# Attention with one quarter-array turn of eight families per step, full-array products alone between, and its first statistics and rows moved up a half round

## The chip, the cores and the metric

The kernel runs on one core of a Trainium2 chip. The core has a matrix engine (TensorE; in the profile PE for its matmuls and PEld for its weight loads), a vector engine (VectorE, DVE), an activation engine (ScalarE, ACT), a general engine (GpSimd, POOL) and a queue that issues most transfers (SyncE, SP). Each engine works through its own list of instructions, and semaphores make an instruction wait for another engine's. The metric is the time of one execution on the device in microseconds (us); lower is better. In the profile every instruction carries the line of the kernel that made it.

## The reference

Three residual blocks on x of shape 2 x 2048 x 256: a gated scan, a feed-forward network with ternary weights, an attention of second order, and the feed-forward network again. The change is in the attention and in what leads into it and out of it.

```
x = x + gated_scan(layernorm(x))
x = x + ffn(layernorm(x))
x = x + hla(layernorm(x))          # 16 heads of 64
x = x + ffn(layernorm(x))

def hla(x):                        # per batch and head
    q, k, v = x @ W_q, x @ W_k, x @ W_v
    for t:
        G   += k_t (k_t . C)       # with C before this t
        S   += k_t k_t^T
        C   += q_t v_t^T
        o_t  = q_t (S C - G)
    return o @ W_o
```

S C - G is the sum over i <= t of u_i v_i^T with u_i = S(i) q_i, so the attention is two linear attentions in a row: first u from q and the running sum S of k k^T, then o from q and the running sum M of u v^T.

## The kernel before

**Order.** The engines' orders are written out by hand: inside the attention each of PE, DVE, ACT and POOL executes its instructions in the order in which the program makes them. All tokens stay in on-chip memory (`x_sb`). `front` (from L555) runs the scan and the first feed-forward network, block by block; `attention` follows; then the second feed-forward network runs over the eight blocks of 512 tokens. Its first block is worked in among the last steps of the attention by the class `Last`.

**Steps.** The attention goes over 32 steps s: 16 chunks n of 128 tokens, each for batch 0 (even s) and batch 1 (odd s). Eight families of 32 matmuls belong to a step. Every matmul uses a quarter of the array (64 rows, 64 columns), four at a time:

- `inter(s, "S", "uT")`, `products(s, "kT", "p1")`, `intra(s, "S", "kN", "p1", "uT")` make u: what earlier chunks give, the masked products of k and q, what this chunk gives. `update(s, "kN", "kN", "S")` adds the chunk to S.
- `update(s, "uN", "vN", "M")` adds the chunk to M, and `inter(s, "M", "oT")`, `products(s, "uT", "p2")`, `intra(s, "M", "vN", "p2", "oT")` make o the same way.

DVE takes `products` out of PSUM under the mask (L838) and adds `update` to the sums (L901). `evict` (L870 on) copies u and o out of PSUM in three copies, on ACT or DVE. k and u are needed turned as well: `keys_out`/`units_out` transpose 32x32 squares on DVE (L260) and write them to DRAM, `turn_rows` reads them back (both on SP's queue), and `turn_end` (for u: `units_end`) copies them into place on ACT (L931).

**Products.** Between the quarter-array families PE runs full-array (128x128) matmuls: `outward` (L912), which multiplies o by W_o in two halves of 3 and 5, and the projections. `Seven` computes one projection (k, q or v) of a whole chunk of both batches with seven products instead of eight; `go(1)` to `go(7)` issue them, `go(0)` is an addition alone. They share two or three PSUM banks: `X` holds product 1; product 6 is added into the same bank after ACT has copied product 1 out, then 7 after ACT has copied 6 out, then 4 after DVE has added 7 elsewhere. k is projected in even steps (seven products), q and v in odd ones (fourteen). X and Z of k and q lie in the two banks of the ring "uT", which also holds the two banks of `inter(s, "S", "uT")`; those of v lie in the ring "oT". Four more banks are the ring "ps".

**The order inside a step before.** The families are spread over four places of a step, two at a time, and projections and `outward` lie between them: `inter` and `products` for u; then both `intra`; then `update` of S and M; then `inter` and `products` for o of the step before. ACT's units_end(s-1) lies in an even step at its start, in an odd step between the evictions and the projections; the rows of the next chunk (`norm_rows`, L195) or their turned copy (`norm_end`, L313) come at the end of a step, after `k.go(4)` or `q.go(4)`.

**Lead-in.** The first chunk's rows are normalized and turned through DRAM by three functions, `attention_stats`, `attention_rows` and `attention_turned`, called from `front` as `then[0]`, `then[1]`, `then[2]` in the last of its eight feed-forward rounds. `a_(4)` adds the scan's result of unit 4 to `x_sb` (transposes on PE, L424, and two additions on DVE) ahead of the first round.

## Time and profile before

| what | value |
|---|---|
| time, median of 3 runs | 1082.48 us (1080.03 to 1083.65) |
| the profiled execution's own time | 1081.18 us |
| its span, first to last instruction | 1079.3 us |
| PE busy in the span | 1057.5 us (98%) |
| DVE, ACT, POOL busy | 681.0, 596.4, 175.5 us (63%, 55%, 16%) |
| mean granted TensorE clock | 0.995 |
| `outward` (L912), 512 instructions | 124.0 us busy |
| masked evictions (L838), 128 instructions | 82.1 us busy, 682 ns each |
| turned copies kT and uN (L931), 32 and 31 | 66.7 and 64.6 us busy, 2085 ns each |
| k squares to DRAM and back, median from issue to landing | 3.5 us out, 2.9 us back |
| u squares to DRAM and back | 3.3 us out, 3.1 us back |

The span runs from the first to the last instruction of the profiled execution; the device time is a little longer. "Busy" of PE counts a matmul from its start to the modelled end, so neighbours overlap, and PE's start-to-start distances say more than its busy time. In an f32 row of the timeline "x2" or "x8" counts instruction records: a product of k or v is 2 records of 512 columns, one of q 8 records of 128, a quarter-array family 64 records. The attention's steps run from about 236 us to 956 us of the span; the first of them starts its quarter-array work at 259.9 us.

### The profile page before, as it was taken

The numbers are of one execution on the slowest core, as the hardware profiler recorded it, in microseconds if no ns is written. First come the engines' busy times: TensorE is split into PE (matmuls) and PEld (weight loads), VectorE is DVE, ScalarE is ACT, GpSimd is POOL, SyncE is SP. The second block draws the span as 40 slices with busy tenths as digits, with TensorE's granted clock in tenths as the row PEclk, the third lists the DMA queues.
The fourth block names the chain that finished last, engine by engine and source line by source line (L and its number), as shares of the span: only waits on it lengthen the run. The fifth ranks groups of instructions, "written<-read, shape, count | busy, mean of one in ns | idle before, by whom it ended". The sixth has DMA issues, their size and how long they took to land. (4 is left out here: it accounts for less than half of the span.)

```text
span 1079.3 us, 43538 instructions
## 1 busy us (share of the span) xinstructions
PE 1057.5 (98%) x20024; PEld 817.6 (76%) x20024; DVE 681.0 (63%) x1041; ACT 596.4 (55%) x826; POOL 175.5 (16%) x290
## 2 busy tenths in 40 slices
PE   9989999979999999999999999999999999999998
PEld 7557779866677777777777777777777777789987
DVE  7965556544665757667657576676675665645554
ACT  4446666854555455544554545545545455447875
POOL 3422223831011011010110100101101011013120
PEclk9999999999999999999999999999999999999999
DMA  9220000002433424324333243342342443211011
GB/s 329 96 78 1 1 2 1 1 20 80 139 100 120 135 73 135 128 72 139 102 120 127 79 134 107 95 139 101 121 134 75 133 122 116 62 60 37 24 40 39
DMA packets 71463, 97.58 MB, mean 90 GB/s; under 512 B 7280, under 2 KB 58864, under 8 KB 71024
## 3 DMA queue, kind: packets, MB, share of 16 engines
q1 hardware_dynamic: 69664, 92.43, 26.0%
q8 instruction: 157, 2.57, 1.0%
q10 hardware_dynamic: 1584, 2.36, 0.9%
q14 instruction: 26, 0.21, 0.1%
q0 software_dynamic: 32, 0.00, 0.0%
HBM read 50.99 MB, written 43.78 MB: 88 GB/s over the span
## 5 line engine op out<-in xcount | busy, mean ns | idle before, releaser
L838 DVE TENSOR_TENSOR p<-hp,mask 128x512 f32<-128x512 f32 x128 | 82.1, 682 | 84.9 <-PE hp L832 84.9
L912 PE MATMUL hy<-wo,oT 128*128 128x256 f32 x512 | 124.0, 385 | 0.9 <-PE hqT_X L773 0.5
L204 DVE TENSOR_TENSOR hl<-h,hh 128x1024 fp32r<-128x1024 f32 x60 | 74.2, 1240 | 64.7 <-ACT hh L203 64.6
L912 PEld LDWEIGHTS hy<-wo,oT 128*128 128x128 f32 x512 | 93.6, 190 | 20.3 <-issue 7.7
L502 ACT ACTIVATE h<-h,b_sb 128x512 f32<-128x512 f32 x120 | 77.7, 682 | 49.5 <-PE h L496 49.4
L730 POOL TENSOR_TENSOR S<-xnT 128x128 f32<-128x128 f32 x30 | 13.8, 461 | 512.5 <-ACT xnT L313 512.5
L874 ACT COPY uT<-huT 128x512 f32<-128x512 f32 x32 | 18.7, 585 | 129.4 <-PE huT L863 129.4
L195 ACT ACTIVATE xn<-x_sb,nb,rs 128x256 f32<-128x256 f32 x124 | 65.2, 591 | 18.8 <-POOL nb L181 18.8
L901 DVE TENSOR_TENSOR S<-S,hS 128x512 f32<-128x512 f32 x60 | 41.2, 686 | 42.5 <-PE hS L889 39.5
L931 ACT COPY kT<-rawkT 128x1024 f32<-128x1024 f32 x32 | 66.7, 2085 | 0.0
L260 DVE STREAM_TRANSPOSE sqkT<-kN 128x1024 f32<-128x1024 f32 x32 | 65.8, 2056 | 1.3 <-ACT kN L809 1.2
L260 DVE STREAM_TRANSPOSE squN<-uT 128x1024 f32<-128x1024 f32 x31 | 63.6, 2052 | 4.0 <-ACT uT L876 3.5
L931 ACT COPY uN<-rawuN 128x1024 f32<-128x1024 f32 x31 | 64.6, 2085 | 1.0 <-ACT uT L876 0.7
L203 ACT CAST hh<-h 128x1024 fp32r<-128x1024 f32 x60 | 63.0, 1050 | 1.9
L518 PE MATMUL o<-w2r,hh 128*128 128x256 f32 x256 | 62.0, 284 | 0.0
L518 PE MATMUL o<-w2r_back,hh 128*128 128x256 f32 x248 | 60.3, 284 | 0.9 <-DVE x_sb L527 0.9
L518 PE MATMUL o<-w2r,hl 128*128 128x256 f32 x256 | 60.8, 279 | 0.0
L518 PE MATMUL o<-w2r_back,hl 128*128 128x256 f32 x248 | 59.9, 282 | 0.0
L496 PE MATMUL h<-xh,w1r 128*128 128x512 f32 x128 | 58.6, 458 | 0.0
L809 ACT COPY vN<-hvN_X 128x512 f32<-128x512 f32 x16 | 9.4, 585 | 78.8 <-PE hvN_X L778 78.8
L163 DVE BATCH_NORM_STATS2 st<-x_sb 128x6 f32<-128x256 f32 x128 | 51.4, 402 | 2.3 <-DMA x_sb<-in_x_dram 2.3
L783 DVE TENSOR_TENSOR kN<-kN,hkN_Y 128x512 f32<-128x512 f32 x16 | 11.0, 686 | 64.9 <-ACT kN L792 64.9
(221 smaller groups left out, 2504.7 us busy)
## 6 DMA issues: line engine op xcount, KB each, us to landing
dsqkT<-sqkT SPq DMA_DIRECT2D x32, 512.0 KB, 3.5
rawkT<-dsqkT SPq DMA_DIRECT2D x128, 128.0 KB, 2.9
dsquN<-squN SPq DMA_DIRECT2D x31, 512.0 KB, 3.3
rawuN<-dsquN SPq DMA_DIRECT2D x124, 128.0 KB, 3.1
out_dram<-x_sb SPq DMA_DIRECT2D x15, 256.0 KB, 2.3
x_sb<-in_x_dram SPq DMA_DIRECT2D x7, 512.0 KB, 9.0
dsqxn<-sqxn SPq DMA_DIRECT2D x14, 256.0 KB, 3.7
rawxn<-dsqxn SPq DMA_DIRECT2D x56, 64.0 KB, 2.5
```

Source lines behind the costliest of these rows:

```text
L163: nc.vector.bn_stats(st[:, c, :], x_sb[:, g, :])
L195: nc.scalar.activation(xn[:, c, :], x_sb[:, g, :], AF.Identity, bias=nb[:, c : c + 1], scale=rs[:, c : c + 1],)
L203: copy(hi, src)
L204: nc.vector.tensor_tensor(lo, src, hi, ALU.subtract)
L260: nc.vector.transpose(to, src)
L496: nc.tensor.matmul(ph, lhsT=w1r[:, d, f * P : (f + 1) * P], rhs=r[:, d, :], start=(d == 0 and k == 0), stop=(d == ND - 1 and k == 1),)
L502: nc.scalar.activation(h[:, f % 2, :], ph, AF.Gelu, bias=b1_sb[:, f : f + 1])
L518: nc.tensor.matmul(to, lhsT=h[f // 2][:, f % 2, c * P : (c + 1) * P], rhs=w2r[:, f, :], start=(f == 0 and k == 0 and c % 2 == 0), stop=(f ...
L838: nc.vector.tensor_tensor(d[s][nm][:, h], banks[h], mask8, ALU.mult)
L901: nc.vector.tensor_tensor(t, prev, banks[c], ALU.add)
L912: nc.tensor.matmul(py, lhsT=d[s]["oT"][:, p, :], rhs=wo[:, p, :], start=(p == 0), stop=(p == NPR - 1),)
L931: act(t, d[s]["r" + nm].rearrange("p t q -> p q t"))
```

## The change

Each step starts with all its quarter-array work in one stretch, written as `quarters(s)`; the work for o lags by two steps instead of one (`inter`, `products`, `intra` of s-2 beside those of u of s). After it come the projections, `outward` (both halves of s-2, moved into the same step), the squares and the rows. All evictions of o but the last go on ACT. `update` loses its `between` hook, `products`, `inter` and `evict` take another ring or tag for the last step. The last steps and `Last` are laid out anew: the last two o's are made in one final stretch, and `second_squares` follows it.

```
+        def quarters(s):
+            inter(s, "S", "uT")
+            products(s, "kT", "p1")
+            if s >= 1:
+                units_end(s - 1)
+                update(s - 1, "uN", "vN", "M")
+            if s >= 2:
+                inter(s - 2, "M", "oT")
+                products(s - 2, "uT", "p2")
+            intra(s, "S", "kN", "p1", "uT")
+            evict(s, "uT")
+            if s < NS - 1:
+                update(s + 1, "kN", "kN", "S")
+            if s >= 2:
+                intra(s - 2, "M", "vN", "p2", "oT")
+                evict(s - 2, "oT")
...
         for s in range(NS):
             first, n = s % 2 == 0, s // 2
             more = n + 1 < CPB
-            inter(s, "S", "uT")
-            products(s, "kT", "p1")
...
+            quarters(s)
+            if more and first:
                 k = Seven(n + 1, "kN", "uT")
-                k.go(2)
...
+                k.go(1, 2)
                 units_out(s)
                 turn_rows(s, "uN")
+                k.go(5)
                 if n + 2 < CPB:
+                    stats = norm_stats(norm_pool, pair(n + 2), bias=True)
+                else:
+                    last.stats()
+                k.go(0)
+                outward_(s - 2, 0)
+                k.go(6, 7)
                 turn_end(s + 1, "kT")
...
-                k.go(*((6, 3, 7) if s > 0 else (3,)))
...
+                outward_(s - 2, 1)
+                k.go(3)
+                keys_out(s + 2)
+                turn_rows(s + 2, "kT")
                 k.go(4)
                 if n + 2 < CPB:
                     xn = norm_rows(norm_pool, pair(n + 2), stats)
                 else:
                     last.rows()
+                    last.weights(True)
+            elif more:
+                q, v = Seven(n + 1, "qT", "uT"), Seven(n + 1, "vN", "oT")
+                q.go(2, 1)
+                v.go(2, 1)
+                units_out(s)
+                turn_rows(s, "uN")
+                if n + 2 < CPB:
+                    raw = norm_squares(pool, pair(n + 2), [xn], 2, "xraw", 1)
+                last.part()
+                for i in (5, 0, 6):
+                    q.go(i)
+                    v.go(i)
+                last.part()
+                outward_(s - 2, 0)
+                turn_end(s + 1, "kT")
+                q.go(7)
+                v.go(7)
+                last.part()
+                keys_out(s + 2)
+                turn_rows(s + 2, "kT")
+                outward_(s - 2, 1)
+                q.go(3)
+                v.go(3)
+                last.part(None)
+                q.go(4)
+                v.go(4)
+                if n + 2 < CPB:
+                    xnT = norm_pool.tile([P, ND, B * P], FP, tag="xnT", bufs=1, name=f"xnT{n + 2}")
+                    pairs[n + 2] = norm_end(raw, xnT)
+                    pair_sums(n + 2)
+                else:
+                    last.weights(False)
+                    last.turned()
+            elif first:
+                last.begin()
+                last.fill(2)
+                units_out(s)
+                turn_rows(s, "uN")
...
+                turn_end(s + 1, "kT")
+                last.second_stats()
...
             else:
+                last.fill(1)
                 outward(s - 2, 0)
-        last.out()
-        last.second_squares()
-        outward(NS - 3, 1)
+                outward(s - 2, 1)
+                units(s)
+                last.second_rows()
+                last.fill(1)
+        inter(NS - 2, "M", "oT")
+        products(NS - 2, "uT", "p2")
+        update(NS - 1, "uN", "vN", "M")
+        inter(NS - 1, "M", "oT", "uT")
+        products(NS - 1, "uT", "p2", "p1")
         intra(NS - 2, "M", "vN", "p2", "oT")
         evict(NS - 2, "oT")
...
+        intra(NS - 1, "M", "vN", "p2", "oT")
+        evict(NS - 1, "oT", dve, "uT")
+        last.second_squares()
+        last.out(2)
```

Ahead of the first step, v's product 4 and the turning of the next chunk's rows move out of step 0, and the second chunk of k is read back earlier:

```
         keys_out(1)
+        turn_rows(1, "kT")
...
         v.go(3, 7)
+        v.go(4)
+        pairs[1] = norm_turned(norm_pool, pair(1), xn, bufs=1)
+        pair_sums(1)
```

In `front`, `a_(4)` goes behind the first products and the first matmuls of round 0 (for that `scan_room` is split into `scan_gate` and `scan_pair`), and the three calls for the attention's first chunk move up by about half a round:

```
         t_(5)
-        a_(4)
         two_rings()
...
-                for _ in range(4):
+                for j in range(4):
                     run(products, 1)
                     run(steps, 1)
+                    if i == 0 and j == 0:
+                        a_(4)
...
-            if not more:
+            if i == NB - 2:
                 then[0]()
...
-            if not more:
+            if i == NB - 2:
+                then[1]()
+            elif not more:
                 wo = const.tile([P, NPR, D], FP, tag="wo", name="wo")
                 nc.sync.dma_start(out=wo, in_=w_o.rearrange("(c p) e -> p c e", p=P))
-                then[1]()
+                then[2]()
...
-                else:
-                    then[2]()
```

More of the change, by code (lines that the diff above doesn't have):

```diff
@@ L376, in scan_part @@
         pa, pkv, pq = ps
-        a, kq = scan_room(pool, g0, e)
+        a, kq = scan_gate(pool, g0, e), scan_pair(pool, g0, e)
         nc.scalar.activation(a[:, :nt], pa, AF.Sigmoid)
@@ L392, in product @@
             return pq
-        room = [scan_room(pool, g0, e) for e in range(ND)]
+        gate = [scan_gate(pool, g0, e) for e in range(ND)]
         for e in range(ND):
-            nc.scalar.activation(room[e][0], product(2, e), AF.Sigmoid)
+            nc.scalar.activation(gate[e], product(2, e), AF.Sigmoid)
         yield
         for e in range(ND):
-            a, kq = room[e]
+            a, kq = gate[e], scan_pair(pool, g0, e)
             kv = product(1, e)
@@ L406, in scan_steps, with scan_gate, scan_pair @@
             yield
-    def scan_room(pool, g0, e):
-        a = pool.tile([P, BT], FP, tag="a", name=f"a{g0}_{e}")
-        return a, pool.tile([P, 2, BT], FP, tag="kq", name=f"kq{g0}_{e}")
+    def scan_gate(pool, g0, e):
+        return pool.tile([P, BT], FP, tag="a", name=f"a{g0}_{e}")
+    def scan_pair(pool, g0, e):
+        return pool.tile([P, 2, BT], FP, tag="kq", name=f"kq{g0}_{e}")
     def scan_line(pool, g0, e, nt, a, kq, kv, last):
@@ L822, in attention, with products @@
         mask8 = mask2.unsqueeze(1).to_broadcast([P, NPR, CH])
-        def products(s, left, nm):
+        def products(s, left, nm, tag=None):
             b, n = steps[s]
@@ L835, in products, with inter @@
                         )
-            d[s][nm] = pool.tile([P, 2, NPR, CH], FP, tag=nm, bufs=1, name=f"{nm}{b}_{n}")
+            d[s][nm] = pool.tile([P, 2, NPR, CH], FP, tag=tag or nm, bufs=1, name=f"{nm}{b}_{n}")
             for h in range(2):
                 nc.vector.tensor_tensor(d[s][nm][:, h], banks[h], mask8, ALU.mult)
-        def inter(s, sums, nm):
+        def inter(s, sums, nm, ring=None):
             b, n = steps[s]
-            banks = [bank([P, NPR, CH], f"h{nm}{b}_{n}_{c}", nm) for c in range(2)]
+            banks = [bank([P, NPR, CH], f"h{nm}{b}_{n}_{c}", ring or nm) for c in range(2)]
             for p in range(NPR):
@@ L868, in intra, with evict @@
                         )
-        def evict(s, nm, copy=act):
+        def evict(s, nm, copy=act, tag=None):
             b, n = steps[s]
             banks = d[s][nm + "b"]
-            t = pool.tile([P, NPR, P], FP, tag=nm, bufs=2 if nm == "uT" else 1, name=f"{nm}{b}_{n}")
+            tag = tag or nm
+            t = pool.tile([P, NPR, P], FP, tag=tag, bufs=2 if tag == "uT" else 1, name=f"{nm}{b}_{n}")
             copy(t[:, :, halves[0]], banks[0])
@@ L877, in evict, with update @@
             d[s][nm] = t
-        def update(s, left, right, sums, between=None):
+        def update(s, left, right, sums):
             b, n = steps[s]
@@ L894, in update @@
             for c in range(len(banks)):
-                if between and c == 1:
-                    between()
                 t = state.tile([P, NPR, DK], FP, tag=f"{sums}{b}", bufs=3, name=f"{sums}{b}_{n}_{c}")
@@ L977, in attention, with outward_ @@
         v.go(3, 7)
+        v.go(4)
[17 more added lines that the diff above has]
+                evict(s - 2, "oT")
+        def outward_(s, half):
+            if s >= 0:
+                outward(s, half)
         for s in range(NS):
@@ L980, in attention @@
             more = n + 1 < CPB
-            inter(s, "S", "uT")
-            products(s, "kT", "p1")
-            if first and n + 2 < CPB:
-                stats = norm_stats(norm_pool, pair(n + 2), bias=True)
-            elif s == NS - 4:
-                last.stats()
-            elif s == NS - 2:
-                last.second_stats()
-            if s == 0:
-                v.go(4)
-                pairs[1] = norm_turned(norm_pool, pair(1), xn, bufs=1)
-                pair_sums(1)
-            if s % 2 == 1 and more:
-                q, v = Seven(n + 1, "qT", "uT"), Seven(n + 1, "vN", "oT")
@@ L995, in attention @@
-            if s == 1:
-                q.go(2)
-                v.go(2)
-                keys_out(s + 1)
-            elif s % 2 == 1 and s + 1 < NS:
-                keys_out(s + 1)
-            if s == 2:
-                k = Seven(n + 1, "kN", "uT")
-                k.go(2)
-            if first and s > 0:
-                units_end(s - 1)
-            if s < NS - 1:
-                last.part()
-            if s >= 3:
-                outward(s - 3, 1)
-            intra(s, "S", "kN", "p1", "uT")
@@ L1011, in attention @@
-            if s >= 2:
-                intra(s - 2, "M", "vN", "p2", "oT")
-            if s + 1 < NS:
-                turn_rows(s + 1, "kT")
-            evict(s, "uT")
-            if not more:
-                if not first:
-                    evict(s - 2, "oT", dve)
-                last.begin(first)
-                fill = last.fill
-                fill(1)
-                if first:
-                    evict(s - 2, "oT", act)
-                else:
-                    units_end(s - 1)
-                    units(s)
-                fill(1)
-            elif first:
-                if s != 2:
-                    k = Seven(n + 1, "kN", "uT" if s > 0 else "oT")
-                    k.go(2)
-                k.go(1)
-                if s >= 2:
-                    evict(s - 2, "oT")
-                else:
-                    units_out(s)
-                    turn_rows(s, "uN")
-                k.go(0, 5)
-                if s == 0:
-                    k.go(6)
-            else:
-                if s >= 2:
-                    evict(s - 2, "oT", dve)
-                if s > 1 or not more:
-                    units_end(s - 1)
+            quarters(s)
@@ L1046, in attention @@
+            if more and first:
+                k = Seven(n + 1, "kN", "uT")
+                k.go(1, 2)
                 units_out(s)
                 turn_rows(s, "uN")
+                k.go(5)
                 if n + 2 < CPB:
-                    raw = norm_squares(pool, pair(n + 2), [xn], 2, "xraw", 1)
-                if s > 1:
-                    q.go(2)
-                    v.go(2)
-                for part in (q, v) if s > 1 else (v, q):
-                    part.go(1)
-                if s == NS - 3:
-                    last.part()
@@ L1057, in attention @@
-                q.go(0, 5)
-                v.go(0, 5)
-                if s == 1:
-                    units_end(s - 1)
-                q.go(6)
-                v.go(6)
-            last.part()
-            if s == NS - 1:
-                last.second_rows()
-            if s + 1 < NS:
-                update(s + 1, "kN", "kN", "S", None if s > 0 else lambda: k.go(7))
-            if s >= 1:
-                update(s - 1, "uN", "vN", "M")
-            if s == NS - 1:
-                update(s, "uN", "vN", "M")
@@ L1072, in attention @@
-            if first and not more:
-                turn_end(s + 1, "kT")
-            if not more:
-                fill(1)
-            elif first:
-                k.go(*((6, 3, 7) if s > 0 else (3,)))
-            else:
-                v.go(7)
-                q.go(7)
-                if s == NS - 3:
-                    last.part()
-                v.go(3, 4)
-                q.go(3)
-            last.part()
-            if first and s > 0:
-                units_out(s)
-            if more:
-                turn_end(s + 1, "kT")
@@ L1090, in attention @@
-            if s >= 1:
-                inter(s - 1, "M", "oT")
-                products(s - 1, "uT", "p2")
-            if not more:
-                fill(1)
-            elif first:
+                    stats = norm_stats(norm_pool, pair(n + 2), bias=True)
[4 more added lines that the diff above has]
+                k.go(6, 7)
+                turn_end(s + 1, "kT")
+                outward_(s - 2, 1)
+                k.go(3)
@@ L1100, in attention @@
                     last.rows()
-            else:
-                q.go(4)
-            if not first and s + 2 < NS:
-                keys_out(s + 2)
-            if first and s > 0:
-                turn_rows(s, "uN")
-            if not first and n + 2 < CPB:
-                xnT = norm_pool.tile([P, ND, B * P], FP, tag="xnT", bufs=1, name=f"xnT{n + 2}")
-                pairs[n + 2] = norm_end(raw, xnT)
-                pair_sums(n + 2)
-            elif s == NS - 3:
-                last.turned()
@@ L1113, in attention @@
-            if s == NS - 4:
-                last.weights(True)
-            last.part()
-            if s == NS - 3:
-                last.part(None)
-                last.weights(False)
-            if s >= 2:
-                outward(s - 2, 0)
-        last.out()
-        last.second_squares()
-        outward(NS - 3, 1)
+                    last.weights(True)
[37 more added lines that the diff above has]
+                turn_rows(s, "uN")
+                last.part()
+                outward(s - 2, 0)
+                last.fill(2)
+                turn_end(s + 1, "kT")
+                last.second_stats()
+                last.part()
+                outward(s - 2, 1)
+                last.fill(2)
+                last.part(None)
+            else:
+                last.fill(1)
+                outward(s - 2, 0)
+                outward(s - 2, 1)
+                units(s)
+                last.second_rows()
+                last.fill(1)
@@ L1124, in attention @@
+        inter(NS - 2, "M", "oT")
[3 more added lines that the diff above has]
+        products(NS - 1, "uT", "p2", "p1")
         intra(NS - 2, "M", "vN", "p2", "oT")
         evict(NS - 2, "oT")
-        last.out()
-        inter(NS - 1, "M", "oT")
-        products(NS - 1, "uT", "p2")
+        intra(NS - 1, "M", "vN", "p2", "oT")
+        evict(NS - 1, "oT", dve, "uT")
+        last.second_squares()
+        last.out(2)
@@ L1129, in attention @@
         outward(NS - 2, 0)
         outward(NS - 2, 1)
-        intra(NS - 1, "M", "vN", "p2", "oT")
-        evict(NS - 1, "oT")
-        last.out()
         last.second_turned()
+        last.out(2)
         outward(NS - 1, 0)
@@ L1212, in halves_room, with begin, out @@
                 return t[:, 0], t[:, 1]
-            tag = (None, "kN", "qT", "vN")[a]
-            return [self.room(tag, [P, 2, BT], f"{t}{a}_", FR) for t in ("hh", "hl")]
-        def begin(self, first):
-            if first:
-                self.hid = Hidden(self.g0, self.halves_room)
-                self.steps = ffn_in(
-                    self.g0, self.rhs, self.hid,
-                    lambda a: const.tile([P, 2, BT], FP, tag="wv_t", name=f"h_last{a}"),
-                )
+            tags = ("kN", "kN") if a == 1 else ("qT", "vN")
+            return [self.room(tag, [P, 2, BT], f"{t}{a}_", FR) for t, tag in zip(("hh", "hl"), tags)]
+        def begin(self):
+            self.hid = Hidden(self.g0, self.halves_room)
+            self.steps = ffn_in(
+                self.g0, self.rhs, self.hid,
+                lambda a: const.tile([P, 2, BT], FP, tag="wv_t", name=f"h_last{a}"),
+            )
         def fill(self, n):
             run(self.steps, n)
-        def out(self):
+        def out(self, n):
             if not hasattr(self, "outs"):
-                self.outs = ffn_out(self.g0, self.hid, True, "uT")
-            run(self.outs, 1)
+                self.outs = ffn_out(self.g0, self.hid, True, "oT")
+            run(self.outs, n)
     by_hand = {
```

## The prediction

> **What bounds the kernel now.** First the busy times: PE works nearly the whole span, the others a little over half of it, so only PE's own work and its waits count. Then PE's waits, longest first.

> ```profile
> PE 1057.5 (98%) x20024; PEld 817.6 (76%) x20024; DVE 681.0 (63%) x1041; ACT 596.4 (55%) x826; POOL 175.5 (16%) x290
> ...
> PE hkN_Y L778 <- ACT xnT_first L313: 5.9, 1, 5.9
> PE py L424 <- DVE kq L380: 3.2, 1, 3.2
> PE hoT L849 <- DVE M L901: 2.1, 1, 2.1
> ...
> PE hM L889 <- ACT uN L931: 1.0, 1, 1.0
> ```

> All waits stand in the lead-in and the last steps; from 350 to 850 us PE waits for no other engine. Third, the timeline of an odd step, to price a turn from full-array to quarter-array work and back.

> ```profile
> 543.95 1.02 PE L778 MATMUL hvN_X<-wv_t,S 128*128 128x512 f32 x2
> ...
> 544.90 1.02 PEld L889 LDWEIGHTS hS<-kN 64*64 64x64 f32 x64 [0.76 <-issue]
> 544.91 1.16 PE L889 MATMUL hS<-kN 64*64 64x64 f32 x64
> ...
> 545.83 1.03 PEld L889 LDWEIGHTS hM<-vN,uN 64*64 64x64 f32 x64
> 545.89 1.11 PE L889 MATMUL hM<-vN,uN 64*64 64x64 f32 x64
> ...
> 546.93 1.12 PE L778 MATMUL hvN_X<-wv,S 128*128 128x512 f32 x2
> ...
> 547.89 1.05 PE L773 MATMUL hqT_X<-S,wq 128*128 128x128 f32 x8
> ```

> From one product's start (543.95) to the end of the next one's issue (547.89) are 3.94 us. Two 512-column products follow each other elsewhere at 0.86, a second family's weight loads start 0.93 after the first's. 3.94 - 2 x 0.86 - 2 x 0.93 leaves 0.36 us for one turn. Last the granted clock, in windows around the two long waits (columns: window, length, PE busy and records, clock, DMA share, GB/s).

> ```profile
> 56.50:59.90 3.40, 0.82 (x8) 1.00 0.00 0
> 59.90:63.30 3.40, 2.81 (x7) 0.50 0.00 0
> 234.00:237.40 3.40, 1.68 (x15) 1.00 0.20 77
> ...
> 240.80:247.70 6.90, 6.09 (x10) 0.51 0.00 0
> ```

> Each long wait is followed by a stretch at half clock.

> **What the change removes.** *Turns:* the trace has 131 stretches of quarter-array matmuls; the new order of PE has 34. 97 x 0.36 = 34.9 us. That is PE's own time, so it counts in full.
> *Lead-in of the attention:* the rows, squares and transfers of the first chunk are issued a half round earlier, behind SP work of that round only; round 7 takes some 15 us on PE (220.6 to 235.7) and the chain from the squares to the copy `xnT_first` took 6.5 us (233.95 to 240.47), so it is hidden. The wait of 5.9 goes. The four groups that ran at half clock started 1.87, 1.71, 1.70 and 1.27 us apart instead of 0.86 to 0.89: 3.1 more. What the earlier rows add on ACT (1.09) and DVE (1.11 and statistics) lies beside PE's round 6; uncovered it would cost 2.2.
> *`a_(4)`:* behind two gate products (4 records each, 3.4 us) and four FFN matmuls, its transposes find kq ready. About 0.4 us for xnT remains of the 3.2, and 1.1 of half clock goes: 3.8. Together 12.8.
> *Waits of the last steps that are laid out anew:* 2.1 + 1.0 + 0.5 + 0.2, and 0.7 for qT in step 2: 4.5.

> **What it adds: product 7 behind product 6.** Before, product 3 stood between:

> ```profile
> 523.30 1.12 PE L778 MATMUL hkN_X<-wk_t,S 128*128 128x512 f32 x2
> ...
> 524.27 1.02 PE L778 MATMUL hkN_Z<-wk,S 128*128 128x512 f32 x2
> ...
> 524.47 0.58 ACT L800 COPY kN<-hkN_X 128x512 f32<-128x512 f32 x1 [1.07 <-PE hkN_X L778]
> ...
> 525.12 1.10 PE L778 MATMUL hkN_X<-wk,S 128*128 128x512 f32 x2
> ```

> Product 7 starts 0.07 after ACT's copy of 6; without product 3 PE would have been there at 524.27. `k.go(6, 7)` makes that 0.85 us of waiting in each of 15 even steps: 12.8. `outward`'s first half, which could cover it, stands before product 6.

> **What it adds: uN comes last on ACT.** In the new order ACT has, one after the other: the copy of the stretch's last product (4), the rows (even) or their turned copy (odd), then `units_end`. PE has after product 4 only `inter` and `products`, then `update` of M, which reads uN.

> ```profile
> 528.18 1.13 PE L778 MATMUL hkN_X<-wk_t,xnT 128*128 128x512 f32 x2
> ...
> 529.35 0.59 ACT L809 COPY kN<-hkN_X 128x512 f32<-128x512 f32 x1 [2.31 <-PE hkN_X L778]
> 529.83 1.09 ACT L195 ACTIVATE xn<-x_sb,nb,rs 128x256 f32<-128x256 f32 x2
> ...
> 555.27 1.15 ACT L313 COPY xnT<-rawxn 128x512 f32<-128x512 f32 x1
> ...
> 556.32 2.09 ACT L931 COPY uN<-rawuN 128x1024 f32<-128x1024 f32 x1
> ```

> Product 4, not being the first of its stretch, ends 1.02 after its start. Then 0.05 to the copy, 0.48 to the next instruction (529.35 to 529.83), 1.05 for rows or turned copy (555.27 to 556.32), 2.09 for uN, 0.05 back to PE: 4.74. PE would be at the update after 0.95 (product with turn) + 0.98 + 0.93 = 2.87. Wait: 1.87 us. In odd steps 0.7 of it falls earlier, because `inter` wants the bank that product 4 is still copied from; the sum is the same. Everything behind the waiting matmul on PE, five families, slides with it. Nothing covers it: in steps 2 to 28, 27 x 1.87 = 50.5. Bounds: 1.6 if the copies follow closer than shown, 2.1 if each hop costs 0.1: 43 to 57.

> Is uN's transfer in time? u's evictions end 9.4 after the step's start, DVE's S additions 10.1, its squares 12.2; out and back took 528.92 to about 536.4 here (issue at 533.3 plus 3.1), 7.4, so it lands at 19.6; an even step lasts 20.0 and ACT asks at 21.6. Two us of slack, in odd steps seven. DVE's other duties (masks, M, S) end 0.3 to 1 us before PE wants them.

> **Ends.** Step 0: product 4 of v right behind product 7 waits for DVE's addition (0.9), `intra` for the mask (1.5). Step 1: its uN has a short step before it (squares until 8.4, landing 15.4 to 15.9, copy to 17.5, update wanted at 13.5): 4.0 to 4.5. Step 29 has twice as many rows, 2.9; step 30 casts instead, 1.0. In step 31 squares of u stand behind the FFN's split on DVE, so uN is some 5.4 late, and `outward` waits 1.4 for o. The final stretch: `inter` of the last o waits for mask and M addition (1.8), its `intra` for the mask (0.5), `out` 0.3. `second_squares` now starts behind the last eviction: transfer (8.6 from 943.06's squares on, by the rows there), cast 2.05 and difference 2.05 end about 2 us after PE wants them. Sum 22; these are rough, 12 to 30.

> **Sum.** 1079.3 - 34.9 - 12.8 - 4.5 + 12.8 + 50.5 + 22 = 1112.4 us of span. The execution took 1.9 more than its span: 1114.3, and the median of the runs stands 1.3 above the profiled execution: I say 1115. Per pair of steps it is 43.1 now, 45.6 then: six turns less (2.1), two uN waits and one product wait more (4.6).

> **The clock.** A window with 0.82 of 3.40 us busy was followed by half clock, one with 1.68 busy was not. A wait of 1.87 leaves at least 1.53 busy, between the two and near the second, so I take full clock; at the other end all 27 waits would cost 1.7 us each, 46. [...]

> **Rivals.**
> - *ACT is in time, and the turns decide (8%).* For it: ACT is busy 55% only, and PE waited for uN once so far, 1.0 us. Against: before, uN's copy ended six to eight us ahead of its reader (558.4 for 566.1); now it stands behind product 4 in the same list. It would give 1112.4 - 50.5 = 1061.9, or 1065 as a median. The point is a wait of about 0.65 us: 1112.4 - 1079.3 = 33.1 too much, 33.1 / 27 = 1.2 less than 1.87.
> - *Break-even (2%)*: the wait comes out at about that point.
> - *The half of it (6%)*: waits of 0.8 to 1.2, 1086 to 1098.
> - *The waits take the clock down as well (13%).* For it: the window above with 0.82 busy. Against: 1.68. With a quarter to all of the 27: 1127 to 1161.
> - *The turns stay.* Excluded: the order of PE shows 34 stretches.

> **Chances and range.** My forecast, 1098 to 1127, has 71%. Slower by over 0.3% (what a measurement of this kernel can tell from no change) is forecast, half and clock: 90%; same 2%; faster 8%. The range 1098 to 1130 takes in both ends of the uN wait (-7, +6), of the product wait (0.65 to 0.9: -3, +1), of the ends (-10, +8) and the lowest part of the clock case.

> **What will show it.** Right: PE's list of waits is led by hM waiting for ACT's uN, near 55 us in some 30 waits; hkN_X waits for ACT's kN 15 times, 12.8 us; no wait for `xnT_first`, no half clock at 240 us. Wrong: hM waits for a transfer, or for 0.6 and less; a clock below 1.00 between 260 and 900 us; steps of a pair less than 44 us apart.

## The result, and the profile after

| | before | after |
|---|---|---|
| time, median of 4 runs each | 1082.89 us (1080.03 to 1083.65) | 1236.88 us (1235.78 to 1240.47) |
| span of the profiled execution | 1079.3 us | 1238.7 us |
| PE busy | 1057.5 us (98%) | 1059.5 us (86%) |
| mean granted clock | 0.995 | 0.988 |
| first quarter-array matmul of the attention | 259.89 us | 246.56 us |
| a pair of steps in the middle (after: 560.5 to 614.9 us) | 43.1 us | 54.4 us |

The ratio is 1.1433, with an interval of 1.1402 to 1.1465. The prediction said slower and gave 1115, with 1130 as its upper end: the direction held, the size did not. PE has the same matmuls as before and is as busy as before; 14% of the span is now waiting. The list of PE's waits of the kernel after (columns: total us, times, longest) shows for whom:

```profile
PE hM L893 <- ACT uN L933: 43.5, 31, 4.6
PE hS L893 <- issue: 26.1, 15, 2.5
PE hoT L866 <- issue: 25.6, 16, 2.2
PE hp L835 <- issue: 21.3, 15, 1.9
PE huT L866 <- issue: 20.2, 14, 1.9
PE hkN_X L781 <- ACT kN L803: 11.5, 15, 0.8
PE huT L852 <- ACT kN L812: 9.4, 14, 0.7
```

The lines for uN and for the copies of k are the predicted ones. Those that end in "issue" are not: there the profile shows nothing that PE waited for. Over the whole kernel they are 98.4 us in 69 waits; before, they were 1.3 us in 3:

```profile
PE hp L832 <- issue: 0.6, 1, 0.6
PE hqT_Y L773 <- issue: 0.5, 1, 0.5
PE hy L912 <- issue: 0.2, 1, 0.2
```

The timeline of an even step after shows where they lie (columns: start, length, instruction; in brackets the idle time before it):

```profile
560.50 1.16 PE L852 MATMUL huT<-qT,S 64*64 64x64 f32 x64
561.48 1.11 PE L835 MATMUL hp<-qT,kT 64*64 64x64 f32 x64
564.24 1.16 PE L893 MATMUL hM<-vN,uN 64*64 64x64 f32 x64 [1.65 <-ACT uN L933]
565.23 1.11 PE L852 MATMUL hoT<-qT,M 64*64 64x64 f32 x64
566.16 0.65 PE L835 MATMUL hp<-qT,uT 64*64 64x64 f32 x32
568.04 0.64 PE L835 MATMUL hp<-qT,uT 64*64 64x64 f32 x29 [1.24 <-issue]
...
569.50 0.64 PE L893 MATMUL hS<-kN 64*64 64x64 f32 x31
571.50 0.64 PE L893 MATMUL hS<-kN 64*64 64x64 f32 x29 [1.36 <-issue]
```

They do not stand at the head of a family, as the wait for uN at 564.24 does, but in its middle, and they stand a fixed number of records apart: the matmul at 571.50 is the 128th after the one at 568.04. Every matmul here has its own weight load (the page counts 20024 of each), so that is 256 instructions. The page's part on transfers has a queue that the prediction did not look at (packets, MB, share of the transfer engines' time), first before, then after:

```profile
q8 instruction: 157, 2.57, 1.0%
...
q8 instruction: 157, 2.57, 0.9%
```

157 packets and 2.57 MB are 16.4 KB a packet, 64 bytes for each of 256 instructions. PE's 20024 matmuls and as many weight loads would fill 156.4 such packets, so PE's instructions are taken to come in pieces of this size. A border is the place where one piece ends and the next begins. The single packets, from the trace's transfer records (q8), set beside the matmul that starts the piece:

```
packet starts   lands     first matmul of that piece
565.71          566.67    568.04
569.20          570.14    571.50
```

The cycle reads: a piece is begun (568.04), the packet of the next one starts 1.15 later (569.20), takes 0.95, and 1.36 after its landing the first matmul of it runs: 3.46 us. Over the kernel the closest two packets are 3.32 apart. A piece of quarter-array families is used up in two families, 2 x 0.93 = 1.86 us. At that rate four pieces in a row, as a stretch of eight families needs them, cannot come in 7.4 us; behind the first border of a stretch, a border costs about 1.6 by this reckoning (3.46 - 1.86). Before, no stretch had more than two families, 128 records, and so hardly more than one border, with 512-column products behind it that use only 2 records in 0.86 us.

### The profile page after: what moved, and what is told of

The parts are those of the page before. It is cut to its first block, busy times and chain, and to the rows that moved or that the text cites. A ratio compares the mean times of both kernels' runs of the same rounds, so it can differ in the third digit from the quotient of the medians.

```text
span 1238.7 us, 43590 instructions
## 1 busy us (share of the span) xinstructions
PE 1059.5 (86%) x20024; PEld 836.7 (68%) x20024; DVE 663.6 (54%) x999; ACT 621.0 (50%) x868; POOL 172.3 (14%) x290
## 3 DMA queue, kind: packets, MB, share of 16 engines
q8 instruction: 157, 2.57, 0.9%
## 4 chain that ended last, share of the span: by engine, by line
PE 76%; ACT 10%; issue 9%; DVE 2%; DMA 2%; SPq 0%; ACTq 0%; POOL 0%; DVEq 0%; POOLq 0%
PE o L520 9%; PE h L498 9%; PE hy L914 8%; ACT uN L933 5%; PE hkN_X L781 5%; PE hqT_X L776 5%; PE hvN_X L781 4%; PE pq L369 3%; PE pq L389 3%; PE hM L893 3%; PE hoT L866 3%; PE hp L835 3%; PE hS L893 3%; PE huT L866 3%; PE hoT L852 3%
## 5 line engine op out<-in xcount | busy, mean ns | idle before, releaser
L914 PEld LDWEIGHTS hy<-wo,oT 128*128 128x128 f32 x512 | 97.0, 190 | 38.8 <-issue 26.8
L914 PE MATMUL hy<-wo,oT 128*128 128x256 f32 x512 | 120.7, 379 | 1.1 <-ACT oT L880 1.1
L893 PE MATMUL hM<-vN,uN 64*64 64x64 f32 x1984 | 41.3, 226 | 44.8 <-ACT uN L933 43.5
L195 ACT ACTIVATE xn<-x_sb,nb,rs 128x256 f32<-128x256 f32 x124 | 65.1, 592 | 17.1 <-POOL nb L181 17.1
L893 PEld LDWEIGHTS hM<-vN,uN 64*64 64x64 f32 x1984 | 35.8, 138 | 50.2 <-ACT uN L933 47.8
L893 PE MATMUL hS<-kN 64*64 64x64 f32 x1984 | 43.3, 225 | 26.2 <-issue 26.1
L866 PE MATMUL hoT<-p,vN 64*64 64x64 f32 x2048 | 43.8, 228 | 25.6 <-issue 25.6
L175 POOL TENSOR_SCALAR rs<-mv 128x2 f32<-128x2 f32 (+1 forms) x34 | 10.2, 301 | 378.3 <-DVE mv L164 276.1
L903 DVE TENSOR_TENSOR M<-M,hM 128x512 f32<-128x512 f32 x60 | 41.2, 687 | 39.8 <-PE hM L893 36.7
```

Of the source, the lines that this page charges most:

```text
L866: nc.tensor.matmul(banks[c][halves[h ^ c], p, :], lhsT=d[s][nat][halves[c], feats(h, p)], rhs=d[s][pm][halves[c], h, p, :], start=(d[s][su ...
L893: nc.tensor.matmul(banks[c][halves[h], p, :], lhsT=d[s][left][halves[c], feats(h, p)], rhs=d[s][right][halves[c], feats(h, p)], start=True ...
L903: nc.vector.tensor_tensor(t, prev, banks[c], ALU.add)
L914: nc.tensor.matmul(py, lhsT=d[s]["oT"][:, p, :], rhs=wo[:, p, :], start=(p == 0), stop=(p == NPR - 1),)
```

## The experiments

Two theories were set against each other. Theory 1: the supply of instructions limits the long stretch, in pieces as above. Theory 2: the waits come from the new order, from what ACT, DVE and semaphores do in it, and add up with the others. Ratios are to the kernel before.

**The lead-in alone.** The kernel before, with these edits of the change:

```
-        a_(4)
...
+                    if i == 0 and j == 0:
+                        a_(4)
...
-            if not more:
+            if i == NB - 2:
                 then[0]()
```

and `then[1]`, `then[2]` moved in the same way.

> The kernel before with the lead-in of the change alone (the first chunk's statistics, rows and turned copy a half round earlier, the scan's addition of unit 4 behind the first gate product). Both theories: in the profile after, the first quarter-array matmul starts 13.3 us earlier (246.56 for 259.89), and everything behind it is as before, so 1082.9 - 13 = 1070 us (1067 to 1073), no wait for xnT_first.

1068.86 us, 0.9877 (0.9858 to 0.9896). No wait for `xnT_first` is left in its list, and the longest of PE's waits is 2.1:

```profile
PE hoT L850 <- DVE M L902: 2.1, 1, 2.1
PE warm L1245 <- DVE ones L148: 1.0, 1, 1.0
```

This part of the change is worth 13 to 14 us, as the term of 12.8 said, and it is the fastest kernel of this study. Everything else in the change costs 168 us.

**uN copied earlier.** The changed kernel, with ACT's copy of uN moved:

```
             if s >= 1:
-                units_end(s - 1)
+                if s == NS - 1:
+                    units_end(s - 1)
                 update(s - 1, "uN", "vN", "M")
...
                 k.go(4)
+                units_end(s)
...
                 outward_(s - 2, 1)
+                units_end(s)
                 q.go(3)
```

> The changed kernel, with ACT's copy of uN moved up: in even steps ahead of the rows, in odd steps ahead of products 3 and 4. Theory 1 (PE's instructions arrive in pieces of 128 matmuls and 128 weight loads, one every 3.5 us at best, and a stretch of eight families is four such pieces): the 43.5 us that the update of M waits for uN mostly go, but the pieces come no sooner, so the waits marked issue grow from about 98 us by nearly as much; 1227 to 1237 us. Theory 2 (the wait for uN and the waits marked issue are terms that add up): 43 us less, 1194 us (1188 to 1200), the issue waits stay near 98.

1230.18 us, 1.1381 (1.1346 to 1.1416).

```profile
PE hS L893 <- issue: 23.9, 16, 1.9
PE hoT L866 <- issue: 22.6, 16, 2.2
PE hp L835 <- issue: 20.6, 13, 2.2
PE huT L866 <- issue: 19.1, 14, 1.9
PE hM L893 <- issue: 18.7, 15, 2.0
PE hoT L852 <- issue: 18.1, 12, 2.2
...
PE hM L893 <- ACT uN L933: 8.7, 2, 4.5
```

The wait for uN fell by 34.8 us and the issue waits rose by 26.5, to 124.9. Only 6.7 us were gained. While PE waited for uN, the next piece was on its way (in the kernel after, PE stood from 562.59 to 564.24, and a packet ran from 562.02 to 563.21); without that wait PE reaches the border sooner and waits there. The two waits overlap and do not add up, so theory 2's sum (1194) falls here; whether the new order makes the issue waits is tested further down.

**Product 7 later as well.** In the kernel of the last run:

```
+                k.go(6)
                 outward_(s - 2, 0)
-                k.go(6, 7)
+                k.go(7)
```

> The kernel of the run with uN moved up, and in it the first half of outward between products 6 and 7 of k. The wait of 11.5 us for ACT's copy of product 6 stands among full-array products, where the pieces come fast enough. Theory 1: 11 to 12 us less than the run with uN moved up, about 1220 us (1214 to 1227). Theory 2: the same difference, from 1194 to 1182.

1215.92 us, 1.1249 (1.1218 to 1.1280): 14.3 less, the line `hkN_X <- ACT kN L803` fell from 11.5 to 0.8. Here, among full-array products, the wait counted in full, and both theories had said so; this part of the prediction was an additive term, as it had been taken.

**Six families instead of eight.** In the changed kernel `products(s - 2, "uT", "p2")` and `intra(s - 2, "M", "vN", "p2", "oT")` run only while `s < 4`.

> The changed kernel without the masked products of u and q and what is made from them (products p2 and the second half of o, intra) in 28 steps: o is what earlier chunks give, alone. Stretches of six families instead of eight. Theory 1: one piece of 128 matmuls less in each, 28 x 3.5 = 98 us less than 1236.9: 1139 us (1130 to 1150), and one issue wait less in each step. Theory 2 (the families cost their own time, the waits come from elsewhere): 28 x 2 x 0.93 = 52 us less: 1185 us (1175 to 1190).

1128.90 us, 1.0428 (1.0410 to 1.0447): 108 less than the changed kernel, 1.1 us below the range of theory 1 and 46 below that of theory 2.

```profile
PE hM L893 <- ACT uN L933: 43.5, 31, 4.5
PE huT L866 <- issue: 21.4, 16, 1.9
PE hS L893 <- issue: 16.4, 12, 1.8
```

The two families' own time is 52 us. The rest came out of issue waits, 45.3 us in 39 left of 98.4 in 69, about one less in each step; the wait for uN did not move. The two together are 105.

**A stretch made longer in the kernel before.** This takes the new order out of the question. In `products` of the kernel before:

```
-            for p in range(NPR):
+            for p in [p for _ in range(2 if nm == "p1" else 1) for p in range(NPR)]:
```

and with 4 for 2 in a second run.

> The kernel before, in its own order, with the masked products of k and q (32 matmuls) issued twice in each step, the second time over the first with the same values: one of the four stretches of a step has three families, 192 records, instead of two. Theory 1 (pieces of 128 matmuls with their weight loads, one per 3.5 us): 0.93 of own time, and in about half of the steps a second border of a piece falls into the stretch and costs 1.6: 32 x (0.93 + 0.8) = 55 us more than 1082, so 1137 us (1122 to 1148), and some 15 to 20 issue waits. Theory 2 (issue waits come from the changed kernel's order, not from the length of the stretch): 32 x 0.93 = 30 us more, 1112 us, and no issue waits.

> The same with the products issued four times: a stretch of five families, 320 records, 2.5 pieces. Theory 1: 32 x (3 x 0.93 + 1.5 x 1.6) = 166 us more, 1248 us (1225 to 1265), 40 to 50 issue waits of about 1.6. Theory 2: 32 x 2.79 = 89 us more, 1171 us, no issue waits.

Twice: 1136.32 us, 1.0483 (1.0445 to 1.0520), 20.3 us in 17 issue waits. Four times: 1261.04 us, 1.1638 (1.1604 to 1.1672), 74.7 us in 52 (theory 1 had 40 to 50). In the old order, with nothing else moved, the issue waits are 1.3 us with stretches of at most 128 records, 20.3 with one of 192 in each step, 74.7 with one of 320: the length alone makes them. From the timeline of the second run:

```profile
604.70 1.16 PE L849 MATMUL huT<-qT,S 64*64 64x64 f32 x64
605.68 2.26 PE L832 MATMUL hp<-qT,kT 64*64 64x64 f32 x139
609.26 1.97 PE L832 MATMUL hp<-qT,kT 64*64 64x64 f32 x117 [1.32 <-issue]
611.16 2.42 PE L912 MATMUL hy<-wo,oT 128*128 128x256 f32 x10
```

The wait cuts the 256 records of one family's four passes at an arbitrary place, 139 and 117: a border of a piece, not of the program.

**Full-array work inside the stretch.** The kernel with uN earlier; `outward` is now of s-3, in place of its calls behind the stretch, and product 2 of k moves behind product 7:

```
                 update(s - 1, "uN", "vN", "M")
+            outward_(s - 3, 0)
             if s >= 2:
                 inter(s - 2, "M", "oT")
                 products(s - 2, "uT", "p2")
+            outward_(s - 3, 1)
             intra(s, "S", "kN", "p1", "uT")
...
-                k.go(6, 7)
+                k.go(6, 3, 7)
```

> The kernel of the run with uN moved up; outward, now of s-3, stands inside the stretch: its first half behind the update of M, its second behind the products for o, so that the stretch is 3, 2 and 3 families with 1.3 and 2.2 us of full-array work between; product 3 of k stands between 6 and 7 again. Theory 1: while these products run, which are few instructions, the next piece arrives; 3.5 us in a step fall into waits that are there anyway, 60 to 90 per cent of it if borders and products do not always meet, over 29 steps 60 to 90 us, and 11 for product 7: 1230 - 71 to 101, so 1129 to 1159 us, issue waits down from 125 to 35 to 65 us. Theory 2 (a turn is what costs): 2 more turns in each of 29 steps, 21 us, less 11 for product 7: 1240 us.

1175.51 us, 1.0857 (1.0831 to 1.0883). The issue waits fell to 35.2 us, as theory 1 said; the time missed its range by 16.5 us, and a wait came back:

```profile
PE hM L893 <- ACT uN L933: 31.0, 16, 8.5
PE hoT L866 <- issue: 16.1, 14, 1.8
PE hM L893 <- issue: 11.5, 10, 1.8
...
PE hkN_X L781 <- ACT kN L795: 8.1, 12, 0.7
```

ACT stood idle for the transfer of uN in 24 steps (34.4 us by the view of that tile). With `outward` ahead of it, the second half of u starts 11.6 us after its step (600.73 for 589.11) where it was 8.6 (566.21 for 557.58), and the even step is 22.7 us long where it was 24.5, so the squares of u leave later and are wanted sooner. Two more turns in a step, which theory 2 priced at 21 us, came with 55 us less, of which the wait at product 7 explains 11 to 14.

**Four and three stretches in the new order.** Now the update of M, which needs uN, comes last:

```
             inter(s, "S", "uT")
             products(s, "kT", "p1")
+            outward_(s - 3, 0)
             inter(s - 2, "M", "oT")
             products(s - 2, "uT", "p2")
+            outward_(s - 3, 1)
             intra(s, "S", "kN", "p1", "uT")
             update(s + 1, "kN", "kN", "S")
+            for part in ys:
+                part.go(2)
             intra(s - 2, "M", "vN", "p2", "oT")
+            update(s - 1, "uN", "vN", "M")
```

uN is copied ahead of products 3 and 4 in odd steps and after product 4 in even ones, and product 3 of k stands between 6 and 7 again. The run with three stretches has no products 2 in between: `outward`'s halves stand behind `inter` of o and behind `intra` of u.

> The changed kernel's steps (o two steps late, everything of a step at its start, its lead-in and its last steps) with full-array products between each two families: outward's halves of s-3 behind the products of u and behind those of o, product 2 of the projections ahead of the second half of o; the update of M comes last in the step, uN is copied at the end of the step before. Four stretches of two families, 128 records each. Theory 1 (length of a stretch against pieces of 128 matmuls): at most one border of a piece in a stretch, so issue waits of under 15 us in all, pairs of steps of 43 to 44 us, and 1069 us (the run with the lead-in alone) plus what the last steps cost, up to 22: 1085 us (1069 to 1105). Theory 2 (the order itself, o two steps late and one list of ACT, is what costs, the pieces are a symptom): near 1216 and three more turns a step, 1216 + 30 x 3 x 0.36 = 1248 us.

> The same with two of the three gaps: stretches of 3, 2 and 3 families. Theory 1: one turn less in each of 30 steps (11 us less than with four stretches), and in about half of the stretches of three a second border, one wait of about 1.2 us a step, 36 us more: 1085 - 11 + 36 = 1110 us (1090 to 1130), 30 to 40 us of issue waits. Theory 2: 1216 + 30 x 2 x 0.36 = 1238 us.

Four stretches: 1186.55 us, 1.0964 (1.0942 to 1.0987). Three: 1178.69 us, 1.0894 (1.0864 to 1.0923). The waits for issue came out as theory 1 has them or nearly, 9.4 us in 21 and 42.6 us in 45 (30 to 40 expected). Both times missed, by 102 and 69 us. With four stretches these waits stood in the list instead (with three, the first of them is 14.9 us; that run was not taken apart further):

```profile
PE huT L852 <- ACT qT L812: 40.5, 15, 4.2
PE hkN_X L781 <- DVE kN L786: 15.4, 15, 2.1
PE huT L852 <- ACT kN L812: 9.4, 14, 0.7
```

In the odd steps ACT waits for the transfer of uN, and product 4 of q stands behind it in ACT's list:

```profile
584.51 2.03 ACT L933 COPY uN<-rawuN 128x1024 f32<-128x1024 f32 x1 [2.53 <-DMA rawuN<-dsquN]
586.45 0.58 ACT L812 COPY qT<-hqT_X 128x512 f32<-128x512 f32 x1
```

The kernel spent 58.0 us at half clock (mean granted clock 0.975). Time alone could not tell the theories apart here, so the same order was mended at this place:

```
                 update(s + 1, "kN", "kN", "S")
+                units_out(s)
+                turn_rows(s, "uN")
...
-                units_out(s)
-                turn_rows(s, "uN")
...
-                units_end(s)
                 q.go(3)
                 v.go(3)
...
                 q.go(4)
                 v.go(4)
+                units_end(s)
```

> The kernel of the run with four stretches, in which ACT's copies of product 4 of q waited behind uN (40.5 us in 15 odd steps) and product 4 of k waited for DVE's additions (15.4 us). The squares of u now leave DVE inside the stretch, behind the additions to S, and ACT copies uN after product 4. Theory 1: the waits of 40.5 go and half of the 15.4, issue waits stay under 15, and what of half clock followed those waits goes too (58 us of half clock, up to 20 us of time): 1186.5 - 40 - 8 - 5 to 20, so 1118 to 1135 us. Theory 2 (the order costs, in whatever place its wait shows): new waits of the same size, 1175 to 1195 us.

1129.95 us, 1.0427 (1.0397 to 1.0457).

```profile
PE hkN_X L781 <- DVE kN L786: 11.7, 15, 0.8
PE huT L852 <- ACT kN L812: 9.5, 14, 0.7
PE hM L893 <- ACT uN L933: 4.7, 1, 4.7
```

The 40.5 are gone, half clock is down to 10.2 us, as in the kernel before (mean granted clock 0.995 in both), and the issue waits are 12.3. So the changed order, its lag of two steps and its ends kept, lies 107 us below the changed kernel once no stretch is longer than two families, but for six at the two ends. Not all of the 107 is the issue waits: of PE's waits 175.5 us became 52.4, 86 less for issue, 39 less for uN and 11.5 less at product 7, against new ones such as the 11.7 above; and there are 87 more turns, 31 us at 0.36.

The kernel still lies 61 us above the lead-in alone, 63 in the span. Its waits are 52.4 us against 8.2 there, 44 of the 63. The span without these waits, for the same matmuls, is 18.8 us more (1075.7 for 1056.9), of which half clock explains up to 5. Where the rest of it goes was not taken apart and stays open.

## Why the prediction was right or wrong

- **Turns, 34.9 us: right.** There are 34 stretches instead of 131, and a turn costs what it did. Without issue waits in the way (the run with uN earlier) the four distances around a stretch are 0.95, 0.98, 1.04 and 0.97 where 0.86, 0.93, 0.93 and 0.86 hold inside: 0.09 + 0.05 + 0.11 + 0.11 = 0.36.
- **Lead-in, 12.8: right.** 13.3 in the profile (259.89 to 246.56), 13 to 14 in the run that had nothing else, where no half clock is left at all.
- **Product 7 behind product 6, 12.8: right.** It was 11.5 in 15 waits, and 14 when taken away.
- **uN last on ACT, 50.5, and the uN waits of the ends: the mechanism right, the sum wrong.** The lines for hM (31 waits, as forecast) and for huT waiting for product 4 of k are 52.9 us together, against 50.5 and 13.3 of the ends, 63.8. But the prediction let "everything behind the waiting matmul" slide with it, as if nothing else were late. Taken away, the wait of 34.8 us gave 6.7.
- **The step that failed.** The price of a stretch was taken as families times 0.93 plus a turn, and the sum has no term for its length: it stood at nothing, without a reason. The 0.93 is from stretches of two families, where about one border of a piece falls and is covered (1.3 us of issue waits in the kernel before), and no row of the kernel before has a longer stretch. The runs showed a wait for the next piece of instructions in its place, 98.4 us in 69 waits, where the cycle above has about 1.6 at a border: 63 of the borders stand over 1.0 us from the matmul before, these distances are 113 us together, and the span was 126.3 above the predicted 1112.4. The prediction stated bounds for the waits it saw and none for this; it should have asked what a stretch four times as long uses that a short one does not, and the queue with 157 packets, which stands in the profile before too, would have pointed to it.
- **The clock: taken at full, in part wrong.** The kernel after spent 30.7 us at half clock, the one before 10.2; at half speed that is some 10 us more. One of the two longest blocks (271.25 to 278.07 us) follows the wait of 4.6 for uN in step 1, which the prediction had among its ends, but without a price for the clock. The blocks of half clock start at 271.25, 595.51, 813.97 and on, 95 and 64 times 3.413 us apart, and each of them is 3.41 or 6.83 us long, so the windows shown here lie on a grid of 3.41 us (columns: window, length, PE busy and records, then PEld, DVE, ACT, POOL, clock, DMA share, GB/s):

```profile
377.07:380.48 3.41, 1.60 (x108) 1.60 (x112) 0.90 (x2) 0.74 (x2) 0.00 (x0) 1.00 0.47 128
380.48:383.89 3.41, 1.77 (x79) 1.57 (x69) 3.14 (x3) 1.40 (x3) 0.00 (x0) 1.00 0.02 5
...
592.07:595.48 3.41, 0.93 (x64) 0.80 (x60) 1.25 (x2) 1.74 (x3) 0.00 (x0) 1.00 0.54 133
595.48:598.89 3.41, 3.41 (x127) 3.37 (x127) 1.45 (x3) 0.00 (x0) 0.00 (x0) 0.50 0.02 5
974.40:977.81 3.41, 1.48 (x100) 1.34 (x96) 2.35 (x3) 1.75 (x3) 0.00 (x0) 1.00 0.02 5
977.81:981.22 3.41, 3.41 (x54) 3.29 (x45) 1.91 (x2) 1.75 (x3) 0.00 (x0) 0.50 0.47 180
```

A window with 1.60 busy was followed by full clock, those with 0.93 and 1.48 by half. The prediction reckoned with 1.53 left in a window and took full clock for it; of the seven windows of this grid with 1.48 to 1.60 busy, two were followed by half clock and five by full. A clock below 1.00 between 260 and 900 us was one of its signs of being wrong, and four blocks lie there. The rival that let the clock fall with the waits had this right for a few of them.
- **The rivals.** That ACT would be in time and the turns decide (1065) is excluded: taking most of ACT's wait away left 1230. The direction held, but in good part by luck: of the 154 us that the kernel became slower, the larger part is the issue waits, which the forecast did not have.

## What to carry to other kernels

Before small matmuls are gathered into long stretches, count instructions as well as time: records and weight loads, times 64 bytes, against what these runs showed: one piece of 16.4 KB in about 3.5 us (3.46 in the cycle above, 3.32 between the closest packets). In this kernel a stretch of quarter-array families met hardly any wait for instructions as long as it held no more than one piece (128 f32 records with their loads; 1.3 us in all before, 9.4 and 12.3 in the two runs with four stretches), with large matmuls behind it for the rest of the 3.5 us; a turn of 0.36 us is cheaper than a border of 1.6. And a wait that is removed is worth its length only if the work behind it was ready; here a second wait, on the supply, lay under the first, and 34.8 us of waiting less gave 6.7.
